# Attention block: the first chunk's k and q by seven products, the output bias from weighted rows, and a reordered first unit

## The chip, the cores and the metric

The kernel runs on one core of a Trainium2 chip. The metric is the device time of one execution in microseconds (us), as the median of several runs. The engines are TensorE (PE, its weight loads PEld), VectorE (DVE), ScalarE (ACT), GpSimd (POOL) and SyncE (SP, which only starts loads and stores here).

## The reference

The input x is 8 sequences of 1024 rows of 512 numbers, float32. With LN a layer norm without weights:

```python
def attn(x):                       # 16 heads of 32
    Q, K, V = (split_heads(x @ W.T + b) for W, b in ((Wq, bq), (Wk, bk), (Wv, bv)))
    scores = Q @ K.T / sqrt(32) - (i - j)     # causal, and a decay of 1 a step
    return merge(softmax(scores) @ V) @ Wo.T + bo
def ffn(x):                        # rotate by a Hadamard matrix, quantize to 4 bits, ternary weights
    return quantize(x @ H) @ ternary(weight).T
x = x + LN(attn(LN(x)))
x = x + LN(ffn(LN(x)))
```

The decay lets the kernel leave out keys that lie more than one block of 128 rows behind; a general path is taken if a bound on the scores (kept in `allmax`, tested at the end) does not allow that.

## The kernel before

The rows are cut into 16 chunks of 512 (`CT`), two for each sequence, and a chunk into four tiles of 128 rows. For each chunk the kernel needs the normed rows transposed (`xnT`), then k, q and v. For chunks 1 to 15 these three projections are done by a seven-product scheme for matrices cut in 2 x 2 (`class Projections`): `combine` makes sums of blocks of `xnT` in a tile `T` (two operations with `which` 0, one each with 1 and 2), `Weight.combine` and `Weight.replace` make the sums of the weights' blocks (three and two operations on POOL), `product` issues one of the seven products (four matmuls of 128x256 into one PSUM bank), and `drain` adds it from PSUM into the result, in the order `ORDER = (1, 2, 6, 7, 5, 4, 3)`. In the text k6 is k's product 6. Product 1 is drained by ACT (L440, into `u2`), the others by VectorE (L447 to L470).

Chunk 0 is done ahead of the loop, in the lines 694 to 792, by plain projections (`project`, four matmuls of 128x512 each): four of v, four of k, four of q. In between stand the preparation of the next chunk's tiles (generators `ahead_norms`: load, statistics with `rstd` on POOL, normalising on ACT as `xn`, transposing on PE), the scaling of wq on ACT (`prepare_q`), the combining of the weights on POOL, and the generator `prepare` for the feed-forward weights: their mean absolute values (`wscale`, a reduction on VectorE), for each of four blocks a comparison `below`, the ternary block `tern` and a diagonal `wdiag`; eight transposes for each pair of blocks and copies into `ternT`; a product that spreads the scales over rows (`wscale_ps`); and the output bias bo2 = bo + bv Wo, by four matmuls of `wo_sb` with bv broadcast over columns (`bvw`).

The softmax is shifted by a bound instead of a maximum. Squares of k and q (ACT) are summed per head on PE (`nk`, `nq`), the largest is taken (`mk`, `mq`), their product goes on a diagonal, a matmul with ones spreads it (`m_ps`), VectorE takes the largest (`spread`), and POOL makes the square root (pow), three roundings and the two biases (`Projections.shift`, L510 to L515). The first exponentials (L584) need this bias.

The loop goes over chunks and, in each, over eight units: four groups of four heads for each half of the chunk. A unit is `scores` (16 to 24 matmuls and four exponentials), `mask` and `add_keys` on POOL (L595, L609, in a sequence's first half also the copy L613), `values` on PE (L624 for the values, L643 for the sums by ones, which need `both` from POOL) and `divide` on VectorE. Between units stand the next chunk's products and the rest of finished tiles. The scores have one set of PSUM banks, so that a unit's scores wait for the exponentials of the unit before. Everything else on PE shares three banks (`ps_m`, class `Banks`) that go round in turn or are named by `bank`.

The order of each engine's instructions is the order of the program text (`manual_schedule`); each engine works its own queue in that order and waits at semaphores. Loads start in the order of SP's queue, which itself waits for the buffer that a load overwrites.

## Time and profile before

| what | value |
|---|---|
| median of 3 runs | 1402.89 us (1400.15 to 1403.14) |
| profiled execution | 1402.26 us, its span 1400.6 us |
| PE busy | 1364.7 us, 97% of the span |
| DVE, POOL, ACT busy | 1024.6, 907.3, 681.9 us |
| granted PE clock, mean | 0.993 |
| first k projection starts | 24.92 us |
| first scores start | 61.71 us |
| wk, wq, wf, wo: from issue to landing | 5.4, 7.9, 9.7, 12.2 us |

Times in the text are us from the span's start. The page gives for each engine its busy time and share; the windows view gives the same for a stretch of time; the timeline lists instructions with their start, duration, engine, source line (L...), operation, what is written and read, and in brackets the idle time before it and what ended it. A matmul in float32 is shown as two records, so that "x8" is four of them.

### The profile page before, as it was taken

The numbers are of one execution on the slowest core, as the hardware profiler recorded it, in microseconds if no ns is written. First come the engines' busy times: TensorE is split into PE (matmuls) and PEld (weight loads), VectorE is DVE, ScalarE is ACT, GpSimd is POOL, SyncE is SP. The second block draws the span as 40 slices with busy tenths as digits, with TensorE's granted clock in tenths as the row PEclk, the third lists the DMA queues.
The fourth block names the chain that finished last, engine by engine and source line by source line (L and its number), as shares of the span: only waits on it lengthen the run. The fifth ranks groups of instructions, "written<-read, shape, count | busy, mean of one in ns | idle before, by whom it ended". The sixth has DMA issues, their size and how long they took to land.

```text
span 1400.6 us, 34947 instructions
## 1 busy us (share of the span) xinstructions
PE 1364.7 (97%) x14472; PEld 965.8 (69%) x14472; DVE 1024.6 (73%) x2170; ACT 681.9 (49%) x1176; POOL 907.3 (65%) x1285
## 2 busy tenths in 40 slices
PE   9999999999999999999999999999999999999885
PEld 5577777767766777776776777777776777777453
DVE  5467777777777776876777777777777777687686
ACT  3345454545545445544635545454544545443443
POOL 4565758676676757657666675857657675764554
PEclk9999999999999999999999999999999999999898
DMA  6010011111011011101101101101101101100010
GB/s 227 8 47 24 25 47 46 32 39 47 24 46 47 24 47 47 47 24 47 47 24 46 47 24 47 47 25 46 47 24 47 46 25 47 32 31 17 32 39 33
DMA packets 31750, 58.23 MB, mean 42 GB/s; under 512 B 4064, under 2 KB 4448, under 8 KB 31584
## 3 DMA queue, kind: packets, MB, share of 16 engines
q1 hardware_dynamic: 30720, 54.87, 11.7%
q8 instruction: 116, 1.90, 0.6%
q10 hardware_dynamic: 864, 1.05, 0.2%
q14 instruction: 50, 0.41, 0.1%
HBM read 39.13 MB, written 16.78 MB: 40 GB/s over the span
## 4 chain that ended last, share of the span: by engine, by line


## 5 line engine op out<-in xcount | busy, mean ns | idle before, releaser
L584 ACT ACTIVATE pr<-s,bias 128x512 f32<-128x512 f32 (+1 forms) x512 | 295.8, 661 | 138.0 <-PE s L570 138.0
L609 POOL TENSOR_TENSOR both<-pr 128x1024 f32<-128x1024 f32 (+1 forms) x125 | 262.9, 2103 | 5.3
L153 PE MATMUL o_ps<-wo_sb,oT 128*128 128x512 f32 x512 | 236.5, 605 | 0.6
L595 POOL TENSOR_SCALAR_AFFINE_SELECT pr<-pr 128x1024 f32<-128x1024 f32 x128 | 150.3, 1174 | 100.2 <-ACT pr L584 96.0
L153 PEld LDWEIGHTS o_ps<-wo_sb,oT 128*128 128x128 f32 x512 | 93.2, 192 | 95.6 <-issue 92.8
L187 DVE TENSOR_TENSOR y<-o_ps,bo 128x512 f32<-128x512 f32 x64 | 44.2, 691 | 150.4 <-PE o_ps L153 150.4
L624 PE MATMUL av<-pr,v 128*32 128x128 f32 (+1 forms) x2816 | 130.7, 316 | 1.8 <-POOL pr L595 0.9
L570 PE MATMUL s<-qT,kT 32*64 32x192 f32 (+2 forms) x5632 | 120.4, 286 | 1.5 <-ACT pr L584 1.5
L570 PEld LDWEIGHTS s<-qT,kT 32*64 32x64 f32 x5632 | 100.2, 131 | 31.2 <-issue 21.8
L141 ACT ACTIVATE xn<-xc,nmr,rstd_n 128x512 f32<-128x512 f32 x60 | 48.8, 814 | 140.4 <-POOL nmr L139 140.4
L119 POOL TENSOR_SCALAR rstd_a<-mv_a 128x1 f32<-128x1 f32 x64 | 14.0, 218 | 138.9 <-DVE mv_a L127 137.6
L226 ACT ACTIVATE wT<-h_ps 128x512 f32<-128x512 f32 x64 | 38.2, 597 | 134.7 <-PE h_ps L218 134.7
L212 ACT COPY wT<-wT_ps 128x512 f32<-128x512 f32 x64 | 37.5, 586 | 129.9 <-PE wT_ps L210 129.9
L624 PEld LDWEIGHTS av<-pr,v 128*32 128x32 f32 x2816 | 74.6, 109 | 35.6 <-POOL ca L191 1.3
L238 DVE TENSOR_REDUCE sc<-h_ps 128x1 f32<-128x512 f32 x64 | 44.1, 689 | 65.1 <-ACT wT L226 65.1
L119 POOL TENSOR_SCALAR rstd_c<-mv_c 128x1 f32<-128x1 f32 x64 | 14.7, 230 | 115.3 <-DVE mv_c L127 114.5
L643 PE MATMUL av<-both,ones 128*32 128x256 f32 x1024 | 79.2, 381 | 4.5 <-POOL both L609 4.0
L285 POOL TENSOR_TENSOR y<-y,x 128x512 f32<-128x512 f32 x63 | 80.3, 1274 | 1.4 <-ACT y L284 1.3
L218 PEld LDWEIGHTS h_ps<-had_sb,wT 128*128 128x128 f32 x512 | 67.5, 194 | 6.4 <-ACT wT L212 3.4
L218 PE MATMUL h_ps<-had_sb,wT 128*128 128x128 f32 x512 | 69.0, 278 | 2.1 <-ACT wT L212 2.1
L153 PE MATMUL f_ps<-ternT,qiT 128*128 128x512 bf16 x256 | 65.8, 379 | 2.4 <-ACT qiT L257 2.4
L194 DVE SCALAR_TENSOR_TENSOR x<-y,rstd_a,xr 128x512 f32<-128x512 f32 x64 | 50.8, 793 | 16.4 <-POOL rstd_a L120 16.2
(214 smaller groups left out, 3087.9 us busy)
## 6 DMA issues: line engine op xcount, KB each, us to landing
xr<-in_x SPq DMA_DIRECT2D x64, 256.0 KB, 3.0
out<-y SPq DMA_DIRECT2D x63, 256.0 KB, 2.0
xc<-in_x SPq DMA_DIRECT2D x60, 256.0 KB, 2.8
wv_sb<-in_wvT ACTq DMA_DIRECT2D x4, 256.0 KB, 5.4
x<-in_x SPq DMA_DIRECT2D x4, 256.0 KB, 5.2
wk_sb<-in_wkT SPq DMA_DIRECT2D x1, 1024.0 KB, 5.4
wq_sb<-in_wqT SPq DMA_DIRECT2D x1, 1024.0 KB, 7.9
wf_sb<-in_wf SPq DMA_DIRECT2D x1, 1024.0 KB, 9.7
```

The costliest lines, as they stand in the source:

```text
L141: nc.scalar.activation(xn, xc, AF.Identity, bias=nmr, scale=r)
L153: nc.tensor.matmul(ps, lhs(k), rhs(k), start=(k == 0), stop=(k == KD - 1))
L187: nc.vector.tensor_tensor(y, ps, bo2, ALU.add)
L194: nc.vector.scalar_tensor_tensor(x1, y, ra, xr, ALU.mult, ALU.add)
L218: nc.tensor.matmul(xh[:, k * P : (k + 1) * P], wT[:, k, :], had_sb if k else had0_sb, start=True, stop=True,)
L285: nc.gpsimd.tensor_tensor(y2, y2, x1, ALU.add)
L570: nc.tensor.matmul(s[half * hp : (half + 1) * hp, hh, column[which] + c0 : column[which] + c1], kc.kT[hsl, g, k0 : k0 + hp], ch.qT[hsl, g, ...
L584: nc.scalar.activation(pr[:, :, r0:, own, cols], s5[:, :, r0:, own, cols], AF.Exp, bias=ch.bias[:, own, h : h + 1],)
L595: nc.gpsimd.affine_select(out=own, in_=own, compare_op=ALU.is_ge, fill=0.0, base=0, pattern=[[0, HPG], [0, 2], [1, P]], channel_multiplier=-1,
L609: engine.tensor_tensor(self.both[:, :, r0:], pr[:, :, r0:, 0, :], pr[:, :, r0:, 1, :], ALU.add)
L624: nc.tensor.matmul(av[hh * HD : (hh + 1) * HD, 0, qc : qc + w], kc.v[:, at, h * HD : (h + 1) * HD], pr[:, hh, sc : sc + w], start=(at_part ...
L643: nc.tensor.matmul(av[hh * HD : (hh + 1) * HD, 1, :], ones[:, :HD], self.both[:, hh].rearrange("p r c -> p (r c)"), start=True, stop=True, ...
```

## The change

Four things change, all at the start of the program.

1. k and q of chunk 0 are made by `Projections` like those of the other chunks: seven products each, with `T` made on VectorE, wk's and wq's block sums earlier on POOL, and wq scaled by ACT two tiles earlier. wv's block sums move behind. The steps of `prepare` are cut finer and stand between the products; the fourth tile of chunk 1 is transposed after `nq`.
2. The mean absolute values of the feed-forward weight are made by four ACT operations with an accumulated sum instead of one reduction on VectorE. The output bias is made from rows of Wo weighted by bv on POOL (seven operations) and one matmul with ones.
3. The last four operations of the first `shift` go to VectorE.
4. In chunk 0, the first tile statistics of the loop stand ahead of the first unit, and for the units 0 and 2 a product of the next chunk stands ahead of `values`.

```diff
                 elif which == 1:
-                    nc.gpsimd.tensor_tensor(self.t[:, 2], b22, b12, ALU.subtract)
+                    engine.tensor_tensor(self.t[:, 2], b22, b12, ALU.subtract)
                     self.parts[7] = self.t[:, 2]
                 else:
-                    nc.gpsimd.tensor_tensor(self.t[:, 3], self.t[:, 1], b21, ALU.subtract)
+                    engine.tensor_tensor(self.t[:, 3], self.t[:, 1], b21, ALU.subtract)
                     self.parts[4] = self.t[:, 3]
...
-            def shift(self):
+            def shift(self, engine=nc.gpsimd):
                 ch = self.ch
                 shift = small.tile([P, 1], F32, tag="shift", name=f"shift_{ch.n}")
                 nc.gpsimd.tensor_tensor(shift, spread_max(self.diag, ch.n), half1, ALU.pow)
-                nc.gpsimd.tensor_scalar(shift, shift, -SLACK, -0.5, ALU.mult, ALU.add)
-                nc.gpsimd.tensor_scalar(shift, shift, ROUND, None, ALU.add)
-                nc.gpsimd.tensor_scalar(shift, shift, ROUND, None, ALU.subtract)
+                engine.tensor_scalar(shift, shift, -SLACK, -0.5, ALU.mult, ALU.add)
+                engine.tensor_scalar(shift, shift, ROUND, None, ALU.add)
+                engine.tensor_scalar(shift, shift, ROUND, None, ALU.subtract)
                 ch.bias = small.tile([P, 2, 2], F32, tag="bias", name=f"bias_{ch.n}")
-                nc.gpsimd.tensor_scalar(ch.bias, decay_cols, shift, None, ALU.add)
+                engine.tensor_scalar(ch.bias, decay_cols, shift, None, ALU.add)
...
-        ch.kT = big.tile([P, KD, CT], F32, tag="kT", name=f"kT_{ch.n}")
-        ch.qT = big.tile([P, KD, CT], F32, tag="qT", name=f"qT_{ch.n}")
-        ch.v = big.tile([P, TPC, D], F32, tag="v", name=f"v_{ch.n}")
+        first = Projections(ch, None)
...
-        def squares_of_q(o0, o1):
-            nc.scalar.activation(sqq[:, o0:o1, :], ch.qT[:, o0:o1, :], AF.Square)
+        def squares_of(dst, blocks, cols):
+            nc.scalar.activation(dst[:, blocks, cols], ch.qT[:, blocks, cols], AF.Square)
...
-        first = Projections(ch, None)
         prep = prepare(pools, wf_sb)
-        ahead_steps = {0: "01", 1: "02", 2: "0", 3: "132", 4: "1", 5: "23", 6: "2", 7: "3", 8: "3"}
-        for i in range(3 * KD):
-            if i % 2 or not i:
-                for t in ahead_steps.get(i, ""):
-                    next(ahead_norms[int(t)])
-            which, o = divmod(i, KD)
-            if which == 0:
-                project_v(pools, wv_sb, ch.v, ch.xnT, o, ch.n)
-            elif which == 1:
-                project_qk(pools, "k", wk_sb, bk_sb, ch.kT, ch.xnT, o, ch.n)
-            else:
-                project_qk(pools, "q", wq_sb, bq_sb, ch.qT, ch.xnT, o, ch.n)
-            if i == 0:
+        def go(*which):
+            for t in which:
+                next(ahead_norms[t])
+        for t in range(TPC):
+            if t == 0:
+                go(0, 1)
+            elif t == 1:
+                go(0, 2)
+            elif t == 3:
+                go(1, 3, 2)
+            project_v(pools, wv_sb, ch.v, ch.xnT, t, ch.n)
+            if t == 0:
                 transposed(1)
                 normalised(3)
                 transposed(2)
-            elif i == 1:
+                weights[1].combine()
+            elif t == 1:
                 transposed(3)
-            elif i == KD - 1:
                 prepare_q(wq_sb)
+                weights[1].replace()
                 nc.gpsimd.tensor_tensor(bqk_step[:, 0], bq_sb[:, HB:], bq_sb[:, :HB], ALU.subtract)
                 nc.gpsimd.tensor_tensor(bqk_step[:, 1], bk_sb[:, HB:], bk_sb[:, :HB], ALU.subtract)
-                weights[2].combine()
-                weights[2].replace()
-                weights[1].combine()
-            elif i == 2 * KD - 1:
+            elif t == 2:
+                go(0)
+                for kind in range(3):
+                    first.combine(kind, nc.vector)
+            else:
                 weights[0].combine()
-                weights[1].replace()
-                sqk = squares(ch, "k", ch.kT)
-                sqq = row.tile([P, KD, CT], BF16, tag="sq", name=f"sqq_{ch.n}", bufs=1)
-            elif i == 2 * KD:
+                weights[0].replace()
+                next(prep)
+        kinds = len(Projections.ORDER)
+        first.done = kinds
+        for i in range(kinds):
+            first.product()
+            first.drain()
+            if i in (0, 2, 4):
+                go((1, 2, 3)[i // 2])
+            elif i in (1, 3):
+                go((2, 3)[i // 2])
+            next(prep)
+        sqk = squares(ch, "k", ch.kT)
+        first.done = 0
+        sqq = row.tile([P, KD, CT], BF16, tag="sq", name=f"sqq_{ch.n}", bufs=1)
+        for i in range(kinds):
+            first.product()
+            first.drain()
+            if i == 1:
                 ch.mk = largest_of(ch, "k", norms_of(ch, "k", sqk))
-            elif i == 2 * KD + 2:
-                squares_of_q(0, HB)
-            if i and i % 2 == 0:
-                for t in ahead_steps.get(i, ""):
-                    next(ahead_norms[int(t)])
-            if i in (KD, 6, 2 * KD):
+            elif i == 4:
+                squares_of(sqq, slice(0, HB), slice(0, HW))
+            elif i == 5:
+                squares_of(sqq, slice(HB, KD), slice(0, CT))
+            if i == 0:
                 next(prep)
-        squares_of_q(HB, KD)
+        squares_of(sqq, slice(0, HB), slice(HW, CT))
+        weights[2].combine()
+        weights[2].replace()
+        bank(1)
         next(prep)
+        bank(2)
         next(prep)
+        bank(1)
         ch.mq = largest_of(ch, "q", norms_of(ch, "q", [sqq[:, o, :] for o in range(KD)]))
         first.multiply()
+        bank(0)
         next(prep)
-        first.shift()
+        bank(2)
+        go(3)
+        bank(1)
+        first.shift(nc.vector)
         next(prep)
-        weights[0].replace(nc.vector)
...
+                if at == u == 0:
+                    norm = next(norms_due)
+                    steps(norm, 1)
                 new = Unit(ch, before, u)
...
-                norm = next(norms_due)
-                steps(norm, 1)
+                if at or u:
+                    norm = next(norms_due)
+                    steps(norm, 1)
...
+                late = at == 0 and u < NG
+                if not late:
+                    unit.values()
                 if u >= 4:
                     held, one, two = one, two, held
                 bank(held)
                 proj.product()
+                if late:
+                    unit.values()
                 steps(rest_b, 1)
...
-        nc.vector.tensor_reduce(ws, w, AX.X, ALU.add, apply_absolute_value=True)
+        below = row.tile([P, D], F32, tag="y", name="absolute", bufs=1)
+        for k in range(KD):
+            nc.scalar.activation(below, w[:, k, :], AF.Abs, accum_out=ws[:, k : k + 1])
         nc.vector.tensor_scalar(ws, ws, 1.0 / D, SCALE_MIN, ALU.mult, ALU.max)
...
+        def less(k):
             below = row.tile([P, D], F32, tag="y", name=f"below_{k}", bufs=1)
             nc.vector.tensor_scalar(below, w[:, k, :], lo[:, k : k + 1], None, ALU.is_lt)
+            belows[k] = below
...
-        terns = [ternary(k) for k in range(2)]
-        yield
-        for k in range(2):
-            transposed(k, terns[k])
-        terns += [ternary(k) for k in range(2, KD)]
-        yield
+        less(0)
+        yield
+        ternary(0)
+        yield
+        less(1)
+        yield
+        ternary(1)
+        transposed(0)
+        yield
+        less(2)
+        yield
+        ternary(2)
+        transposed(1)
+        yield
+        less(3)
+        bvw = row.tile([P, D], F32, tag="wT", name="bvw", bufs=1)
+        nc.gpsimd.tensor_scalar(bvw, wo_sb[:, 0, :], bvT_sb[:, 0:1], None, ALU.mult)
+        for k in range(1, KD):
+            more = row.tile([P, D], F32, tag="w", name=f"bvw_{k}", bufs=1)
+            nc.gpsimd.tensor_scalar(more, wo_sb[:, k, :], bvT_sb[:, k : k + 1], None, ALU.mult)
+            nc.gpsimd.tensor_tensor(bvw, bvw, more, ALU.add)
+        yield
+        ternary(3)
         nc.vector.tensor_copy(had0_sb, had_sb)
         nc.vector.memset(had0_sb[:, 0:1], 0.0)
-        bvw = row.tile([P, KD, P], F32, tag="wT", name="bvw", bufs=1)
-        nc.vector.tensor_copy(bvw, bvT_sb.unsqueeze(2).to_broadcast([P, KD, P]))
         yield
         pr = pools.ps_m.tile([P, D], F32, tag="pm", name="wscale_ps")
         nc.tensor.matmul(pr, ones, diag.rearrange("p k q -> p (k q)"), start=True, stop=True)
         nc.vector.tensor_copy(wscale_row, pr)
         yield
+        ps = pools.ps_m.tile([P, D], F32, tag="pm", name="bo2_ps")
+        nc.tensor.matmul(ps, ones, bvw, start=True, stop=True)
+        nc.vector.tensor_tensor(bo2, ps, bo2, ALU.add)
+        yield
+        pt = pools.ps_m.tile([P, 2, KD, P], BF16, tag="pm", name="ternT_ps_2")
         for k in range(2, KD):
-            transposed(k, terns[k])
-        yield
-        ps = pools.ps_m.tile([P, D], F32, tag="pm", name="bo2_ps")
-        for k in range(KD):
-            nc.tensor.matmul(
-                ps, bvw[:, k, :], wo_sb[:, k, :], start=(k == 0), stop=(k == KD - 1)
-            )
-            if k == KD // 2 - 1:
-                yield
-        nc.vector.tensor_tensor(bo2, ps, bo2, ALU.add)
+            for i in range(KD):
+                nc.tensor.transpose(
+                    pt[:, k - 2, i, :], terns[k][:, i * P : (i + 1) * P], ident_bf
+                )
+        yield
+        for k in range(2, KD):
+            nc.vector.tensor_copy(ternT[:, :, k * P : (k + 1) * P], pt[:, k - 2])
         yield
```

More of the change, by code (lines that the diff above doesn't have):

```diff
@@ L691, in start_rest, with bank @@
             )
+        def bank(at):
+            pools.ps_m.named = at
         x0 = big.tile([P, TPC, D], F32, tag="pr", name="x0")
@@ L814, in band @@
         rests_due = ahead(start_rest(ch, t) for ch in chunks for t in range(TPC))
-        def bank(at):
-            pools.ps_m.named = at
         held, one, two = 0, 1, 2
@@ L871, in band @@
                 new.scores()
-                unit.values()
+                late = at == 0 and u < NG
+                if not late:
+                    unit.values()
                 if u >= 4:
@@ L1189, in prepare, with ternary @@
         diag = row.tile([P, KD, P], F32, tag="u", name="wdiag", bufs=1)
-        def ternary(k):
+        belows, terns = {}, {}
+        yield
+        def less(k):
             below = row.tile([P, D], F32, tag="y", name=f"below_{k}", bufs=1)
             nc.vector.tensor_scalar(below, w[:, k, :], lo[:, k : k + 1], None, ALU.is_lt)
+            belows[k] = below
+        def ternary(k):
             tern = row.tile([P, D], BF16, tag=("qi", "qiT")[k % 2], name=f"tern_{k}", bufs=1)
             nc.vector.scalar_tensor_tensor(
-                tern, w[:, k, :], hi[:, k : k + 1], below, ALU.is_gt, ALU.subtract
+                tern, w[:, k, :], hi[:, k : k + 1], belows[k], ALU.is_gt, ALU.subtract
             )
@@ L1200, in ternary, with transposed @@
             )
-            return tern
-        def transposed(k, tern):
+            terns[k] = tern
+        def transposed(k):
             pt = pools.ps_m.tile([P, KD, P], BF16, tag="pm", name=f"ternT_ps_{k}")
             for i in range(KD):
-                nc.tensor.transpose(pt[:, i, :], tern[:, i * P : (i + 1) * P], ident_bf)
+                nc.tensor.transpose(pt[:, i, :], terns[k][:, i * P : (i + 1) * P], ident_bf)
             nc.vector.tensor_copy(ternT[:, :, k * P : (k + 1) * P], pt)
-        terns = [ternary(k) for k in range(2)]
+        less(0)
         yield
-        for k in range(2):
-            transposed(k, terns[k])
-        terns += [ternary(k) for k in range(2, KD)]
+        ternary(0)
         yield
+        less(1)
[17 more added lines that the diff above has]
+        ternary(3)
         nc.vector.tensor_copy(had0_sb, had_sb)
         nc.vector.memset(had0_sb[:, 0:1], 0.0)
-        bvw = row.tile([P, KD, P], F32, tag="wT", name="bvw", bufs=1)
-        nc.vector.tensor_copy(bvw, bvT_sb.unsqueeze(2).to_broadcast([P, KD, P]))
         yield
```

## The prediction, made before the changed kernel was run

> **What bounds the kernel now.** First the page, part 1, for the engine that is nearly always busy:

> ```profile
> PE 1364.7 (97%) x14472; PEld 965.8 (69%) x14472; DVE 1024.6 (73%) x2170; ACT 681.9 (49%) x1176; POOL 907.3 (65%) x1285
> ```

> TensorE (PE) has 36 us of idle in 1400.6. The edits touch the start alone, and the chain of waits is empty in this trace, so next come the windows of that start (columns: length, then busy us of PE, PEld, DVE, ACT, POOL):

> ```profile
> 24.90:55.50 30.60, 30.39 (x89) 14.01 (x88) 18.02 (x25) 13.19 (x20) 21.47 (x22) 1.00 0.07 20
> 55.50:61.70 6.20, 5.87 (x25) 2.66 (x23) 2.78 (x7) 1.74 (x2) 1.01 (x3) 1.00 0.00 0
> 61.70:70.20 8.50, 8.31 (x113) 6.23 (x113) 4.40 (x8) 3.80 (x8) 5.65 (x9) 1.00 0.01 3
> ```

> Row one is the k and q projections, row two the tail up to the first scores, row three the first unit. PE is full, at a granted clock of 1.00, while DVE has 12.6 us free and ACT 17.4 in row one. Work taken off PE here ends the start earlier, until another engine is late, and the loop behind, full on PE too, moves with it. Third, PE's timeline for prices:

> ```profile
> 45.20 10.46 PE L153 MATMUL q_ps<-xnT,wq_sb 128*128 128x512 f32 x24
> 55.50 1.02 PE L1221 MATMUL wscale_ps<-wdiag,ones 128*128 128x512 f32 x2
> 57.85 1.98 PE L1229 MATMUL bo_ps<-wo_sb,bvw 128*128 128x512 f32 x4
> 59.89 1.88 PE L1229 MATMUL bo_ps<-wo_sb,bvw 128*128 128x512 f32 x4
> 61.71 0.77 PE L570 MATMUL s<-qT,kT 32*64 32x192 f32 x32
> 62.41 3.72 PE L417 MATMUL q_ps<-xnT,wq_sb 128*128 128x256 f32 x16
> 68.38 1.99 PE L417 MATMUL q_ps<-T,wq_s 128*128 128x256 f32 x8
> 70.21 0.60 PE L145 MATMUL xnT_ps<-ident,xn 128*128 128x128 f32 x4
> ```

> Starts are what counts, as ends overlap. Three projections run from 45.20 to 55.50: 3.43 each. Two of the seven products run from 62.41 to 66.06 (the next scores): 1.82 each; back to back (70.64 to 72.37) 1.73. Last, what DVE pays beside POOL:

> ```profile
> 28.36 1.25 DVE L1188 TENSOR_SCALAR wscale_lo<-wscale 128x4 f32<-128x4 f32 x1
> 29.64 1.57 DVE L1193 TENSOR_SCALAR below<-wf_sb,wscale_lo 128x512 f32<-128x512 f32 x1
> 39.62 0.48 DVE L1193 TENSOR_SCALAR below<-wf_sb,wscale_lo 128x512 f32<-128x512 f32 x1
> 28.30 1.29 POOL L366 TENSOR_TENSOR wv_s<-wv_s,wv_sb 128x512 f32<-128x512 f32 x1
> 29.66 1.27 POOL L367 TENSOR_TENSOR wv_s<-wv_sb,wv_s 128x512 f32<-128x512 f32 x1
> 62.05 0.32 POOL L515 TENSOR_SCALAR bias<-decay_cols,shift 128x4 f32<-128x4 f32 x1
> 62.66 2.00 ACT L584 ACTIVATE pr<-s,bias 128x256 f32<-128x256 f32 x4 [5.18 <-PE s L570]
> ```

> The same 128x512 operation costs 0.48 alone and 1.57 beside a POOL operation of two inputs, and a 128x4 one 1.25. Drains of PSUM never vary (the group of L447: 691 to 693 ns).

> **PE's own saving.** Eight projections, 8 x 3.43 = 27.4, become 14 products at 1.77 (between 1.73 and 1.82), 24.8: 2.6 saved. The bias row's four products took (59.67 - 57.85) + (61.71 - 59.89) = 3.64; one is left, priced by the wscale product (55.50 to 56.36), 0.86: 2.8 saved. Sum 5.4, the most that can be gained. Transposes only move.

> **Up to the last k drain.** k1 starts where k started, 24.92. ACT copies v until 25.7, then does the four new Abs with sums. No row has an Abs; a Square with a sum (L226) spends 0.49 + 0.19 to the next, so 0.68 each, or 0.85 if each waits for the one before it: done at 28.4 to 29.1. The drain of k1 (0.86) is queued behind them, so its bank comes free at 29.3 to 30.0, and PE reaches k6 at 24.92 + 1.77 + 0.44 + 1.82 = 28.95: 0.7 lost.

> VectorE then has, from about 28.9 (wscale waits for Abs): seven k products' drains 5.0 (0.69 each, 0.87 for k7, 1.3 for k5's two), three tiny scalings 0.5, three below/tern/diag groups at 0.47 + 0.75 + 0.28 = 4.5, stats 0.9, two ternT copies 0.8: 11.7, ending at 40.6 without a wait. PE's own order ends k3 at 24.92 + 7 x 1.77 + 0.7 + two transposes 0.88 + two ternT sets 0.6 = 39.5, and 40.4 with k3's drain. So both are level, and VectorE's waits decide. Twelve of its operations there have two SBUF inputs or are SBUF to SBUF scalings, the kind that waited. In the trace nine of them (27.11 to 35.82) took 8.7 us for 3.5 us of work: 0.58 each. Twelve times 0.58 is 7.0, the far bound: 47.6. But POOL's long work (wq's five, 26.3 to about 33) meets the first four to six, whose delay falls before k6 ends at 31, where VectorE must wait for PE anyway; then POOL itself waits for the statistics of the fourth tile. Three more (at 39 to 41) meet the weighted rows: 3 x 0.58 = 1.7. I take 1.5 as not absorbed: the last k drain D = 42.1, between 40.6 and 47.6.

> [...]

> **From D to the first scores.** Two Squares of k 1.99 and q1's drain 0.86 stand on ACT ahead of q6: 45.0. Five products (q6 to q3) 8.9: 53.9. wscale and bias row 1.7: 55.6, which hides q3's drain (0.69) and the last Square (0.6). nq's result 0.62 later, 56.2; largest 0.69, product 0.19, diagonal 0.28: 57.4, behind which the eight ternT and the moved tile transpose (1.05) are hidden; m_ps 0.22: scores at 57.6 = D + 15.5. Before, 61.71: gain 4.1.

> **The first unit.** Before, scores to the transpose behind q6 took 70.21 - 61.71 = 8.5. After, with S the scores: m_ps, spread 0.29, pow 0.57, then four scalings on VectorE at 0.19 (L502's spacing; POOL took 61.13 to 62.37, 1.24), so bias at S + 2.0 where it was S + 0.66; exp until S + 4.1; mask, sum and copy on POOL (1.11 + 1.28 + 0.61) until S + 7.35. PE: scores 0.7, two products 3.65, scores 0.7, the product put ahead 1.82, values 0.95: the sums are reached at S + 7.8, so nothing waits. Without that reordering they would be reached at S + 6.0 and wait 1.35, so it repays the late bias, and 0.19 that the trace shows at 67.81. The product put ahead needs T of the next chunk: after bias come two ternT copies, the statistics moved in front (0.9) and T (1.3), S + 5.0, against PE at S + 5.05. Level again, and T has two SBUF inputs, beside POOL's rstd and mask: between 0 and 1.3 lost, I take 0.4. The other `late` pass and the loop: nothing.

> **Hidden at no cost.** T of the first chunk on VectorE: 2.8 plus four waits of 0.58 from 18.5, done by 23.6, due at 29. wk's five on POOL from its landing (8.23 + 5.4 = 13.6), 7.1, due at 29 and 31. wq's scaling on ACT, 2.19 from 18.5 (landed 16.6), ends 0.5 before v's copy at 21.25; any excess delays that copy's bank. Weighted rows: four one-input operations between 0.61 (L613) and 1.51 (L373) and three at 1.27, 6.3 to 9.9, from about 37, due at 54.8. wv's five behind them (7.1) end near 54, ahead of pow at 58; that cover is 4 us, and beyond it each us delays the bias. SP: the loads queued behind the third and fourth tile wait for ACT's reads near 31 and 38 (before 30.4 and 41.9), so they are no later.

> **Sum.** 4.1 - 0.4 = 3.7. The profiled execution took 1402.26 (span 1400.6 plus 1.66): 1398.6. The median shown, 1402.89, is 0.63 above it: 1399.2. A measurement of this kernel tells about 0.2%, 2.8 us.

> **Rivals.**
> Slower: VectorE becomes the bound of the k products, because each of the twelve operations pays its 0.58 and nothing absorbs it. Scores come at D + 15.5, so it decides from D = 46.2 - 0.4 = 45.8 on; at 47.6 the loss is 1.4 + 0.4 = 1.8, 1404.7. For it: the 8.7 us for 3.5 us. Against: drains don't wait, and POOL idles in the middle. Chance 0.17.
> No change: half the waits stay (D = 44.1, gain 2.1) and T's wait in the first unit is 1.3: gain 0.8, 1402.1; with one of the two, about 1401. Chance 0.15.
> All hidden: D = 40.6, no loss in the unit, gain 5.4, 1397.5. Chance 0.13. The work does leave PE, since PE's instructions in the built program show 56 products of 128x256 for 32 of 128x512, so "does nothing" isn't a rival.

> The forecast (D between 41 and 43, gain 2.8 and more) keeps 0.55. Faster 0.68, same 0.15, slower 0.17. The range runs from 1396.3 (all hidden, with 1.2 for the spread of three runs, 1400.15 to 1403.14) to 1404.2, which leaves out the far part of the slower case.

> **What would show it.** Right: first scores near 57.6; k6 starting 0.5 to 1 late after the drain of k1; the last k drain at 41 to 43; `both` of the first unit no longer waited for. Wrong: a k drain (L447 to L470) starting more than 1.5 us after its product, with below or tern ahead of it at over 1 us; D beyond 45; PE idle ahead of the first unit's products for T; ACT's Abs above 0.9 each.

## The result, and the profile after

The changed kernel took 1399.42 us (median of 9 runs, 1396.03 to 1400.46), the kernel before 1403.14 (9 runs, 1400.15 to 1403.63): ratio 0.9975, 95% interval 0.9966 to 0.9984. A second measurement gave 1398.01 (10 runs) against 1402.12 (17 runs), ratio 0.9974 (0.9965 to 0.9983). So it is faster by 0.25%, with an interval that leaves 1 out, and close to the forecast (1399.2). The profiled execution took 1398.69, its span 1397.0, which is 3.6 less than before. Only 2.7 of that is made where the change was forecast to make all 3.7.

The page's first part for the kernel after: PE is busy 6.5 us less and still fills 97%. 1.7 of the 6.5 is a spell of lower clock near 1300 us in the kernel before, and not work (see below).

```profile
PE 1358.2 (97%) x14514; PEld 974.7 (70%) x14514; DVE 1035.5 (74%) x2190; ACT 681.0 (49%) x1181; POOL 917.9 (66%) x1290
```

The windows of the start, with the bounds used for before (length, then busy us of PE, PEld, DVE, ACT, POOL):

```profile
24.90:55.50 30.60, 28.41 (x136) 23.07 (x135) 23.44 (x41) 11.41 (x22) 25.70 (x24) 1.00 0.08 23
55.50:61.70 6.20, 5.65 (x63) 4.03 (x62) 4.49 (x14) 2.12 (x5) 1.64 (x2) 1.00 0.00 0
61.70:70.20 8.50, 7.85 (x83) 5.53 (x82) 4.35 (x9) 4.79 (x10) 7.96 (x9) 1.00 0.10 34
```

In the first row PE idles 2.2 us where it idled 0.2, and VectorE and GpSimd are busier by 5.4 and 4.2: work left PE, and PE now waits a little for the other engines. PE's timeline, after:

```profile
29.57 1.97 PE L417 MATMUL k_ps<-T,wk_s 128*128 128x256 f32 x8 [0.44 <-POOL wq_s L365]
32.98 1.97 PE L417 MATMUL k_ps<-T,wk_sb 128*128 128x256 f32 x8 [1.01 <-DVE kT L447]
39.66 1.97 PE L417 MATMUL k_ps<-xnT,wk_s 128*128 128x256 f32 x8 [0.43 <-DVE u_k L466]
45.56 1.96 PE L417 MATMUL q_ps<-T,wq_s 128*128 128x256 f32 x8
58.13 0.46 PE L525 MATMUL m_ps<-diag,ones 128*128 128x128 f32 x2 [0.55 <-DVE diag L519]
58.52 0.77 PE L570 MATMUL s<-qT,kT 32*64 32x192 f32 x32
67.00 0.64 PE L643 MATMUL av<-both,ones 128*32 128x256 f32 x8 [0.64 <-POOL both L613]
67.57 0.66 PE L145 MATMUL xnT_ps<-ident,xn 128*128 128x128 f32 x4
```

Three products of k wait (k6, k7, k3), then PE runs through to `m_ps`. For k6 the profile names GpSimd's `wq_s`, but that was done at 29.25; ScalarE's drain of k1, which frees the PSUM bank, ended at 29.48, and the wait is gone in the run where that drain comes earlier (reduce_dve). The scores start at 58.52 (before 61.71, 3.19 earlier), the transpose behind them at 67.57 (70.21, 2.64 earlier): the first unit gives 0.55 back, at the sums (L643), which wait for `both`. VectorE's timeline, after:

```profile
29.39 1.25 DVE L1223 TENSOR_SCALAR wscale_lo<-wscale 128x4 f32<-128x4 f32 x1
30.67 1.57 DVE L1230 TENSOR_SCALAR below<-wf_sb,wscale_lo 128x512 f32<-128x512 f32 x1
32.16 0.68 DVE L447 TENSOR_TENSOR kT<-k_ps,u_k 128x512 f32<-128x512 f32 x1
41.97 0.68 DVE L470 TENSOR_TENSOR kT<-k_ps,u_k 128x512 f32<-128x512 f32 x1
```

This is the wait of k7: the drain of k2 (L447) stands behind a 128x4 scaling of 1.25 and a comparison of 1.57, both beside GpSimd's sums for wq. The last k drain ends at D = 42.65. And GpSimd's and ScalarE's timelines where the first unit loses:

```profile
60.49 1.99 ACT L584 ACTIVATE pr<-s,bias 128x256 f32<-128x256 f32 x4 [2.28 <-DVE bias L515]
61.97 0.57 POOL L119 TENSOR_SCALAR rstd_n<-mv_n 128x1 f32<-128x1 f32 x1 [2.40 <-DVE mv_n L127]
62.62 0.98 POOL L120 TENSOR_TENSOR rstd_n<-rstd_n,neghalf 128x1 f32<-128x1 f32 x1
63.92 1.11 POOL L595 TENSOR_SCALAR_AFFINE_SELECT pr<-pr 128x1024 f32<-128x1024 f32 x1
```

The exponentials end at 62.48, but the mask starts at 63.92: GpSimd has the three `rstd` operations of the moved statistics in its queue ahead of it, and these wait 2.40 for `mv_n`, which VectorE computes behind the bias and two copies.

**The remaining microsecond.** At the first `o_ps` the kernel after is 2.69 ahead, and matching the 128 units one by one shows 2.70 at 100 us and 3.13 at 1290 us, a slow drift of this pair (the second profile of the same kernel shows 2.86 and 2.74, so no property of the change). The rest comes near 1300 us, where the last chunk has no next products to fill PE. Before, then after:

```profile
1300.20 0.99 PE L570 MATMUL s<-qT,kT 32*64 32x192 f32 x48 [1.49 <-ACT pr L584]
1301.91 5.35 PE L153 MATMUL o_ps<-wo_sb,oT 128*128 128x512 f32 x8
```

```profile
1297.07 0.99 PE L570 MATMUL s<-qT,kT 32*64 32x192 f32 x48 [1.49 <-ACT pr L584]
1298.77 3.65 PE L153 MATMUL o_ps<-wo_sb,oT 128*128 128x512 f32 x8
```

The wait is the same, 1.49, and the same eight records take 5.35 and 3.65: the granted clock was 0.74 from 1300 to 1304 before, 1.00 after. That is 1.70 of lead, of which 1.25 goes again by 1333 (0.92 of it a wait of `wT_ps` for VectorE that the second profile hasn't). 2.70 + 0.43 + 1.70 - 1.25 = 3.58. So of the profiled pair's 3.6, 2.7 belong to the change. The fall of the clock near 1300 is in four of the 14 profiles of this case (before, shift_pool, bias4, wq_later), so it isn't the old kernel's alone. The medians differ by 3.7 and 4.1; what their further microsecond is made of isn't shown, as only single executions have a profile. More time at a lower clock in the kernel before doesn't seem to be it: in the second measurement the runs' mean granted clock averages 0.9938 for both kernels.

### The profile page after: what moved, and what is told of

Same layout as the page of the kernel before. It is cut to its first block, busy times and chain, and to the rows that moved or that the text cites. A ratio compares the mean times of both kernels' runs of the same rounds, so it can differ in the third digit from the quotient of the medians.

```text
span 1397.0 us, 35074 instructions
## 1 busy us (share of the span) xinstructions
PE 1358.2 (97%) x14514; PEld 974.7 (70%) x14514; DVE 1035.5 (74%) x2190; ACT 681.0 (49%) x1181; POOL 917.9 (66%) x1290
## 3 DMA queue, kind: packets, MB, share of 16 engines
q10 hardware_dynamic: 864, 1.05, 0.2%
## 4 chain that ended last, share of the span: by engine, by line
## 5 line engine op out<-in xcount | busy, mean ns | idle before, releaser
L584 ACT ACTIVATE pr<-s,bias 128x512 f32<-128x512 f32 (+1 forms) x512 | 295.3, 660 | 134.6 <-PE s L570 132.3
L153 PE MATMUL o_ps<-wo_sb,oT 128*128 128x512 f32 x512 | 235.5, 603 | 0.6
L153 PEld LDWEIGHTS o_ps<-wo_sb,oT 128*128 128x128 f32 x512 | 93.0, 192 | 94.8 <-issue 91.9
L570 PE MATMUL s<-qT,kT 32*64 32x192 f32 (+2 forms) x5632 | 120.5, 286 | 1.5 <-ACT pr L584 1.5
L570 PEld LDWEIGHTS s<-qT,kT 32*64 32x64 f32 x5632 | 100.3, 131 | 30.6 <-issue 20.7
L226 ACT ACTIVATE wT<-h_ps 128x512 f32<-128x512 f32 x64 | 38.2, 597 | 135.0 <-PE h_ps L218 135.0
L238 DVE TENSOR_REDUCE sc<-h_ps 128x1 f32<-128x512 f32 x64 | 44.1, 689 | 65.2 <-ACT wT L226 65.2
L643 PE MATMUL av<-both,ones 128*32 128x256 f32 x1024 | 79.2, 381 | 4.6 <-POOL both L609 4.0
L153 PE MATMUL f_ps<-ternT,qiT 128*128 128x512 bf16 x256 | 66.0, 381 | 2.4 <-ACT qiT L257 2.4
L146 ACT COPY xnT<-xnT_ps 128x512 f32<-128x512 f32 x60 | 35.2, 586 | 61.0 <-PE xnT_ps L145 61.0
```

Of the source, the lines that this page charges most:

```text
L153: nc.tensor.matmul(ps, lhs(k), rhs(k), start=(k == 0), stop=(k == KD - 1))
L238: nc.vector.tensor_reduce(sc, xh, AX.X, ALU.max, apply_absolute_value=True)
L570: nc.tensor.matmul(s[half * hp : (half + 1) * hp, hh, column[which] + c0 : column[which] + c1], kc.kT[hsl, g, k0 : k0 + hp], ch.qT[hsl, g, ...
L584: nc.scalar.activation(pr[:, :, r0:, own, cols], s5[:, :, r0:, own, cols], AF.Exp, bias=ch.bias[:, own, h : h + 1],)
L643: nc.tensor.matmul(av[hh * HD : (hh + 1) * HD, 1, :], ones[:, :HD], self.both[:, hh].rearrange("p r c -> p (r c)"), start=True, stop=True, ...
```

## The experiments

One table for all, since one reading ties them together: D is the end of the last k drain (L470's start plus its duration), and the third tile's statistics show when that tile's load landed, which differs from execution to execution (23.66 to 26.49); GpSimd's sums for wq stand behind it.

| kernel | third tile's statistics | D | first scores | scores - D | first `o_ps` | `o_ps` - scores | time, us |
|---|---|---|---|---|---|---|---|
| before | 24.00 | | 61.71 | | 93.73 | 32.02 | 1402.26 |
| after | 25.79 | 42.65 | 58.52 | 15.87 | 91.04 | 32.52 | 1398.69 |
| after, again | 26.38 | 42.46 | 58.33 | 15.87 | 90.87 | 32.54 | 1398.01, 10 runs |
| no_late | 24.90 | 42.56 | 58.43 | 15.87 | 95.33 | 36.90 | 1403.73 |
| shift_pool | 24.28 | 41.98 | 57.84 | 15.86 | 89.71 | 31.87 | 1398.30 |
| norm_back | 24.45 | 42.14 | 58.01 | 15.87 | 91.23 | 33.22 | 1397.41 |
| reduce_dve | 25.32 | 42.19 | 58.06 | 15.87 | 90.58 | 32.52 | 1397.93 |
| drain_first | 23.66 | 40.46 | 56.33 | 15.87 | 88.85 | 32.52 | 1397.50 |
| drain_first again | 25.13 | 41.01 | 56.89 | 15.88 | 89.43 | 32.54 | 1398.01, 7 runs |
| best | 24.48 | 40.95 | 56.82 | 15.87 | 88.70 | 31.88 | 1397.25, 6 runs |
| wq_later | 24.21 | 42.40 | 59.33 | 16.93 | 93.41 | 34.08 | 1402.19 |
| bias4 | 26.02 | 44.44 | 62.90 | 18.46 | 95.42 | 32.52 | 1403.38 |
| bias4_drain | 25.44 | 42.79 | 61.24 | 18.45 | 93.76 | 32.52 | 1401.47, 10 runs |
| bias_only | 26.49 | | 62.18 | | 96.70 | 34.52 | 1402.72 |

Times without a count are of one execution each and by themselves tell nothing below some 4 us, since the changed kernel scattered from 1396.03 to 1400.46. They come from different chips too: beside no_late, shift_pool, bias4 and bias_only the kernel before took 1404.81, beside drain_first, reduce_dve and wq_later 1406.38, once each. The starts repeat better: at the scores 0.2 between the changed kernel's two profiles, and D lies from 41.98 to 42.65 in the five profiles whose program is the same up to there (after, after again, no_late, shift_pool, norm_back). A shift of D below 0.7 therefore shows nothing by itself. Where the tail is as in the changed kernel, scores come 15.86 to 15.88 us after D, and where the first unit is, `o_ps` 32.52 to 32.54 after the scores. So each edit is priced by which of the columns it moves.

**no_late**: values ahead of the product in all units, as before.

```diff
-                late = at == 0 and u < NG
+                late = False
```

> The changed kernel with `values` ahead of the next chunk's product again in units 0 and 2. Markers: first scores (58.52 us in the changed kernel), the transpose behind the product put ahead (67.57), the first output projection o_ps (91.04; before 93.73). Theory A, the chain from bias over exponentials, mask and `both` sets the first unit: PE reaches the sums at about 64.6 and `both` comes at 66.95 as before, so PE waits about 2.3 there, the product comes after it, and o_ps starts 1.8 later, 92.8. In unit 2 nothing waits. Rival B, only PE's amount of work counts, order does not: o_ps stays at 91.0.

The waits came as theory A has them: 1.43 for the mask and 1.05 for `both`, against 0.64, 1.84 more. But `o_ps` came 4.29 later than in the changed kernel. PE's timeline and two windows (granted clock third from the end):

```profile
64.99 0.86 PE L624 MATMUL av<-pr,v 128*32 128x256 f32 x16 [1.43 <-POOL pr L595]
66.90 1.08 PE L643 MATMUL av<-both,ones 128*32 128x256 f32 x8 [1.05 <-POOL both L613]
67.91 3.78 PE L417 MATMUL q_ps<-T,wq_s 128*128 128x256 f32 x8
```

```profile
67.00:68.00 1.00, 1.00 (x9) 0.19 (x9) 0.00 (x0) 0.00 (x0) 1.00 (x1) 0.50 0.01 2
74.00:76.00 2.00, 2.00 (x11) 1.75 (x10) 0.88 (x2) 0.00 (x0) 0.00 (x0) 1.00 0.00 0
```

After 2.5 us of waits within 3.3 us the clock was at a half from 66.4 to 73.2, and a product took 3.78 instead of 1.99. That is the other 2.5 us. The 1.84 belong to the edit; a fall of the clock came behind such waits in some executions and not in others (near 1300, behind the same wait of 1.49, in one and not in another; see the last section), so the 2.5 are of this execution.

**shift_pool**: part 3 undone, all of the first bound on GpSimd.

```diff
-        first.shift(nc.vector)
+        first.shift()
```

> The changed kernel with the four last operations of the first shift on GpSimd again. Theory A: four operations at 1.24 in all (61.13 to 62.37 in the kernel before) instead of 0.79 (59.61 to 60.40): bias, exponentials, mask and `both` come 0.5 later, the wait for `both` grows from 0.64 to 1.1 and o_ps starts at 91.5. Rival B, the exponentials are covered by the two products in front of them: o_ps stays at 91.0.

`o_ps` came 1.33 earlier than in the changed kernel, beyond both. 0.67 of it is D, though the program up to there is the same (the load came 1.5 earlier; that this is the reason isn't shown), and 0.65 lies in the unit: 31.87 against 32.52.

```profile
62.59 1.11 POOL L595 TENSOR_SCALAR_AFFINE_SELECT pr<-pr 128x1024 f32<-128x1024 f32 x1 [0.46 <-ACT pr L584]
65.88 0.61 PE L643 MATMUL av<-both,ones 128*32 128x256 f32 x8
```

With the bias off VectorE, the statistics there end 1.9 us after the scores' start (3.35 in the changed kernel), GpSimd's `rstd` is done before the exponentials end, and the mask waits for them alone; the sums wait for nothing. The bias itself comes 0.76 later after `m_ps` than on VectorE, which costs 0.31 at the next scores, less than the 0.64 saved. `best` below repeats the 31.88. Part 3 loses 0.65 us in the first unit.

**norm_back**: the moved statistics back behind the first unit's product.

```diff
-                if at == u == 0:
-                    norm = next(norms_due)
-                    steps(norm, 1)
...
-                if at or u:
-                    norm = next(norms_due)
-                    steps(norm, 1)
+                norm = next(norms_due)
+                steps(norm, 1)
```

> The changed kernel with one thing undone: the first tile statistics of the loop stand behind the first unit's product again, as before; the bias is still finished on VectorE. Theory (POOL's three rstd operations, queued ahead of the mask and waiting for statistics that stand behind the bias on VectorE, are what makes `both` late): the mask starts within 0.2 us of the end of the first exponentials, the sums of the first unit (L643) no longer wait for `both`, and from the first scores to the first o_ps it takes 31.8 to 32.0 us, as with the bias on POOL (31.87), where the changed kernel took 32.52. Rival (the late bias itself does it): L643 still waits 0.5 us or more and the stretch stays at 32.4 or more.

Half of each. The mask starts 0.07 after the exponentials and the sums don't wait, as the theory has it, but the stretch is 33.22 where the theory had 31.8 to 32.0; the rival's 32.4 or more is met, for another reason than the rival's:

```profile
62.05 1.11 POOL L595 TENSOR_SCALAR_AFFINE_SELECT pr<-pr 128x1024 f32<-128x1024 f32 x1 [2.98 <-ACT pr L584]
67.33 0.66 PE L145 MATMUL xnT_ps<-ident,xn 128*128 128x128 f32 x4 [1.04 <-ACT xn L141]
```

`rstd` now comes behind the copy L613, so that the normalised tile is late, and PE waits 1.04 for that. The wait for `both` had been the price of an early tile. So the queue's order does hold up `both`, and the statistics must still be early: the bias in front of them on VectorE is the piece to move.

**bias4**: the bias row by four matmuls, as before; its seven GpSimd operations go.

```diff
...
-        nc.tensor.matmul(ps, ones, bvw, start=True, stop=True)
+        for k in range(KD):
+            nc.tensor.matmul(
+                ps, bvw[:, k, :], wo_sb[:, k, :], start=(k == 0), stop=(k == KD - 1)
+            )
```

> The changed kernel with the output bias by four matmuls and the broadcast copy again; nothing of the weighted rows on GpSimd. PE gets 3 x 0.86 = 2.6 more ahead of nq, GpSimd loses seven operations (38.9 to 49.9). Theory A: first scores at 61.1, less what VectorE's operations after 39 no longer wait (up to 0.8): 60.3 to 61.1, and o_ps at 92.8 to 93.6, so that nearly the whole gain of the change is gone. Rival C, the three waits of PE in the k products are what GpSimd's rows cost, and without them it comes out even: o_ps within 0.5 of 91.0.

4.38 later at the scores, neither the 1.8 to 2.6 of the theory nor the rival's even time. The table splits it: 2.59 lie between D and the scores (18.46 against 15.87), which is PE's own part, and 1.79 in D. wv's sums now stand where the weighted rows stood, and `below`, `tern` and `wdiag` ahead of the last drain take 0.98, 1.16 and 1.28 where they took 0.48, 0.74 and 0.63: 1.57 of the 1.79. `o_ps` is 1.69 later than in the kernel before: without the new bias row the rest of the change loses.

**bias4_drain**: the same with the drain of k2 first (as in drain_first below), to see if the mended order takes the 1.79 away.

> The changed kernel with the bias row by four matmuls again (bvw broadcast, as before) and with the drain of k2 ahead of the scalings and the first comparison. It tells what the 4.4 us of the first edit alone were made of. Theory (2.6 us are PE's three further products, and 1.8 the collisions that wv's earlier POOL operations bring to the drains ahead of k7 and k3; the mended order takes these away): k7 waits under 0.2 us, the last k drain ends at 40.5 to 41.5, the first scores start 2.5 to 3.0 us behind those of the kernel with the mended order alone (56.33 and 56.89), at 59.1 to 59.9, and the first o_ps at 91.6 to 92.4: 0.5 to 1.5 us slower than the changed kernel. Rival (wv's operations collide with whatever stands there): scores at 60.6 or later, o_ps at 93.1 or later, as slow as the kernel before.

The theory fell. k7 doesn't wait, but D is 42.79 against 41.01 of the same order with weighted rows: 1.78 again. VectorE's timeline:

```profile
37.68 1.76 DVE L1236 SCALAR_TENSOR_TENSOR tern<-wf_sb,wscale_hi,below 128x512 bf16<-128x512 f32 x1
39.36 1.28 DVE L1239 TENSOR_SCALAR wdiag<-ident,wscale 128x128 f32<-128x128 f32 x1
```

The same two in drain_first_again, where the weighted rows stand beside them:

```profile
37.36 0.74 DVE L1236 SCALAR_TENSOR_TENSOR tern<-wf_sb,wscale_hi,below 128x512 bf16<-128x512 f32 x1
38.02 0.63 DVE L1239 TENSOR_SCALAR wdiag<-ident,wscale 128x128 f32<-128x128 f32 x1
```

GpSimd's three sums for wv (37.63 to 41.90) stand beside the first pair: 1.67 more, ahead of the last two drains. The bias row in its new form is worth 4.35 us here, 2.57 on PE and 1.78 by what it keeps off VectorE. With the old row, seven products and all, the kernel is within 0.1 us of the one before at `o_ps` (93.76 and 93.73), and 0.999 of its time (0.998 to 0.9999).

**bias_only**: the kernel before with the weighted rows and one matmul, nothing else.

```diff
-        bvw = row.tile([P, KD, P], F32, tag="wT", name="bvw", bufs=1)
-        nc.vector.tensor_copy(bvw, bvT_sb.unsqueeze(2).to_broadcast([P, KD, P]))
+        bvw = row.tile([P, D], F32, tag="wT", name="bvw", bufs=1)
+        nc.gpsimd.tensor_scalar(bvw, wo_sb[:, 0, :], bvT_sb[:, 0:1], None, ALU.mult)
+        for k in range(1, KD):
+            more = row.tile([P, D], F32, tag="w", name=f"bvw_{k}", bufs=1)
+            nc.gpsimd.tensor_scalar(more, wo_sb[:, k, :], bvT_sb[:, k : k + 1], None, ALU.mult)
+            nc.gpsimd.tensor_tensor(bvw, bvw, more, ALU.add)
...
-        for k in range(KD):
-            nc.tensor.matmul(
-                ps, bvw[:, k, :], wo_sb[:, k, :], start=(k == 0), stop=(k == KD - 1)
-            )
-            if k == KD // 2 - 1:
-                yield
+        nc.tensor.matmul(ps, ones, bvw, start=True, stop=True)
+        yield
```

> The kernel before with the weighted rows and one matmul for the output bias, nothing else of the change. 2.6 less on PE behind nq. Theory A: first scores come 2.1 earlier (59.6; m_ps then waits 0.5 for the diagonal), but bias only 0.5 earlier, so the sums of unit 0 wait about 2.2 for `both` where they waited 0.19, and o_ps starts 0.5 to 0.8 earlier than 93.73, at 93.0 to 93.2. Rival B, PE's work counts: o_ps at 91.2 to 91.6.

3.0 later than before at `o_ps`, where a gain was expected. The rows end at 60.54 on GpSimd, `bo_ps` waits 0.21 for them. Half of the row's matmuls had stood between `m_ps` and the scores; with them gone the scores follow `m_ps` at once and the exponentials come 3.47 after the scores' start instead of 0.95, as the bias's operations on GpSimd take 2.29 beside VectorE's work on wq and T where they took 1.24. The next scores wait 1.09, the mask's and the sums' waits are 0.41 and 1.05. That makes the stretch from scores to `o_ps` 34.52, 2.5 of the 3.0. The late load is in the other 0.5. With it (26.49 against 24.00) VectorE's ternary steps and GpSimd's sums come 2.5 later, and PE waits where the kernel before did not:

```profile
37.15 0.40 PE L1206 MATMUL ternT_ps<-ident_bf,tern 128*128 128x128 bf16 x4 [0.68 <-DVE tern L1195]
45.91 0.39 PE L333 MATMUL nk<-sqk,head_rows 128*32 128x512 bf16 x2 [1.44 <-ACT sqk L346]
46.86 0.39 PE L333 MATMUL nk<-sqk,head_rows 128*32 128x512 bf16 x2 [0.55 <-ACT sqk L346]
```

These 2.67 take away all of the 2.6 that PE saved, and GpSimd's rows end late for the same reason. So what the row alone is worth in the kernel before, this one execution doesn't show.

**drain_first**, twice: k2's drain ahead of the scalings and the first comparison, the ternary steps one product later.

```diff
-            next(prep)
+            if i:
+                next(prep)
...
-            if i == 0:
+            if i in (0, 2):
                 next(prep)
...
             nc.scalar.activation(below, w[:, k, :], AF.Abs, accum_out=ws[:, k : k + 1])
+        yield
...
-        yield
 
         def less(k):
```

> The changed kernel with the drain of k2 ahead of the scalings and the first comparison on VectorE, and all steps of the ternary weights one product later. In the changed kernel k7 waited 1.01 for that drain and the last k drain ended at 42.65. Theory A, VectorE's work and its waits beside GpSimd set the end of the k products: k7's wait goes, another drain is late in its place, the last k drain ends at 42.2 to 43.2, first scores at 58.1 to 59.1. Rival B, the one badly placed drain is the loss: last k drain 1.0 earlier, first scores at 57.5.

> The drain of k2 ahead of the scalings and the first comparison, once more and timed. Theory (the order on VectorE makes the gain): last k drain ends at 40.3 to 41.2 and k7 does not wait, whatever the load of the third tile does; about 2 us faster than the changed kernel. Rival (the earlier landing, 23.66 against 25.79, made half of it): with a landing near 25.8 the last k drain ends at 41.3 to 42.0, and the time is 1 us faster or less.

D is 40.46 and, with a later load, 41.01: 1.5 to 2.2 earlier than in the changed kernel's two profiles, about 1.0 or more earlier than in any profile with the old order, and k7 doesn't wait in either. Theory A of the first run fell, and its rival's direction was right with twice the size. The repeat is 1.45 earlier than the changed kernel on the same chip; that the earlier load of the first run made its other half isn't shown. VectorE's timeline of the repeat:

```profile
29.35 0.69 DVE L447 TENSOR_TENSOR kT<-k_ps,u_k 128x512 f32<-128x512 f32 x1 [3.31 <-ACT u_k L440]
31.43 1.38 DVE L1231 TENSOR_SCALAR below<-wf_sb,wscale_lo 128x512 f32<-128x512 f32 x1
40.33 0.68 DVE L470 TENSOR_TENSOR kT<-k_ps,u_k 128x512 f32<-128x512 f32 x1
```

The comparison still takes 1.38, with no drain behind it that PE waits for. But the median is the same as the changed kernel's, 1398.01, where the theory had 2 us less. In its profiled execution the lead of 1.44 at `o_ps` is 0.97 from 760 us on, and the rest goes past 1350, where the granted clock was 0.88 and 0.95 in two windows of 10 us, against 1.00 in the changed kernel. Whether the other six runs lost it in the same way isn't known.

**reduce_dve**: one reduction on VectorE instead of four operations on ScalarE.

```diff
-        for k in range(KD):
-            nc.scalar.activation(below, w[:, k, :], AF.Abs, accum_out=ws[:, k : k + 1])
+        nc.vector.tensor_reduce(ws, w, AX.X, ALU.add, apply_absolute_value=True)
```

> The changed kernel with the mean absolute values by one reduction on VectorE instead of four Abs on ScalarE. VectorE is free from 26.7 to 28.8 in the changed kernel; the reduction took 2.25 in the kernel before, so the scalings start at 29.0 instead of 28.78. The drain of k1 is no longer queued behind Abs: k6's wait of 0.5 goes. Theory A, VectorE is the bound: last k drain ends between 42.6 and 43.0, first scores at 58.5 to 58.9. Rival B, ScalarE's queue is the bound: first scores 0.5 earlier, 58.0.

0.46 earlier at the scores, as the rival has it: k6 no longer waits 0.44, k7 waits 1.42 instead of 1.01. The reduction (2.25) fits into VectorE's idle time ahead of the first drain. D scatters by up to 0.7 for one and the same program, so the 0.44 at k6 is shown and what it leaves at the scores is not.

**wq_later**: wq's five sums on GpSimd behind the fifth product of k.

```diff
             else:
-                weights[0].combine()
-                weights[0].replace()
                 next(prep)
...
+            if i == 4:
+                weights[0].combine()
+                weights[0].replace()
             if i in (0, 2, 4):
```

> The changed kernel with wq's five block operations on GpSimd behind the fifth k product, so that GpSimd does nothing long from 28 to 37 and everything behind it comes later. Theory A, the waits of VectorE are GpSimd's operations: the second tiny scaling and the first comparison, 1.25 and 1.57 in the changed kernel, take 0.17 and 0.48, k7 no longer waits, and the k drains up to k5 end about 1.5 earlier; GpSimd, pushed back by about 7, has wv's operations in front of the square root, which starts 4 to 5 later than the largest is ready, and first exponentials move behind 64. Rival C, those durations are VectorE's own (a cold start, a write of four numbers): they stay at 1.25 and 1.57.

The three scalings and the comparison take 0.17, 0.17, 0.16 and 0.49, where they took 0.49, 0.17, 1.25 and 1.57: GpSimd's sums made those times. In this run's timeline of VectorE:

```profile
28.90 0.16 DVE L1224 TENSOR_SCALAR wscale_lo<-wscale 128x4 f32<-128x4 f32 x1
29.09 0.49 DVE L1231 TENSOR_SCALAR below<-wf_sb,wscale_lo 128x512 f32<-128x512 f32 x1
```

The sums then collide further on (D 42.40), and push wv's behind `spread`: pow starts at 61.36, `m_ps` had waited 1.53, the clock fell to 0.50 from 59.6 to 63.0, and `o_ps` came 2.4 later. The first exponentials start at 62.84, not behind 64 as expected.

**best**: drain_first, reduce_dve and shift_pool together.

> The changed kernel with three edits together: the drain of k2 ahead of the scalings and the first comparison (ternary steps one product later), one reduction on VectorE instead of four operations on ScalarE for the mean absolute values, and the first shift on GpSimd. Theory (the gains seen one by one come from the edits: 2.2, 0.5 and 0.65 us at the first o_ps): o_ps at 88.0 to 88.8, about 2.5 to 3 us faster than the changed kernel. Rival (part of the gains was the landing of the third tile's load, which came 1.5 to 2.1 us earlier in two of those executions and moves POOL's operations on wq with it): where that load lands as in the changed kernel's profile (statistics at 25.8), o_ps comes at 89.5 or later and the kernel is at most 1.5 us faster.

D 40.95, unit 31.88: `o_ps` at 88.70, 2.2 earlier than the changed kernel's on the same chip, of which reduce_dve adds next to nothing once the drain is first (40.95 against 41.01). The rival's condition (a load near 25.8) wasn't met. The median is 1397.25, ratio to before 0.9967 (0.9955 to 0.9979), the lowest median here, but only 0.8 below the changed kernel's, with overlapping intervals: the 2.5 to 3 us that the theory had are not there. The profiled spans differ by 2.0.

> The changed kernel itself, on the chip of the two others. Theory (its gain at the first o_ps, 2.7 us, is its own): o_ps between 90.0 and 91.5, and 2.5 to 3.7 us faster than the kernel before. Rival (the landing of the third tile's load moves the end of the start by half its shift, in both kernels): o_ps leaves that range by as much as the landing differs from 25.79, up to 1 us either way.

The changed kernel again came within 0.2 of its first profile at `o_ps`, with the load 0.6 later: by this the rival fell. The gain of 4.1 in the medians lies above the 2.5 to 3.7 that the theory had.

## Why the prediction was right, and where its steps failed

The size was right at 1399.2 against 1399.42, but not for all its reasons: the gain in the start was 2.7, not 3.7, and a microsecond from elsewhere, which the prediction didn't have and the runs don't explain, filled the gap. That was luck.

**PE's saving.** The bias row was put at 2.8 and measured 2.58 (18.45 - 15.87). Products start 1.73 to 1.80 apart, as taken. What the sum didn't have is that the row's GpSimd form keeps wv's two-input sums away from VectorE, 1.8 more. What the seven products' 2.6 came to is not shown, as no run undid them alone; with the old row (bias4, bias4_drain) all the other parts together left `o_ps` 1.69 later than before, or even.

**Up to the last k drain.** D was put at 42.1, between 40.6 and 47.6; it is 42.65 and 42.46. (With D at 40.6 the prediction's own sum would give a gain of 5.6; its 5.4 is PE's saving.) k6 waited 0.44 (0.7 forecast). The spread over single operations was off: the first collisions were counted as absorbed before PE needs VectorE, yet two of them (1.25 and 1.57) stood ahead of k2's drain and cost 1.01 at k7, while the middle was as empty as forecast. This is one of the prediction's own signs of being wrong: k2's drain started at 32.16, 3.0 after its product's end, with a comparison of 1.57 ahead of it. D still came out near 42.1, since the three operations at 39 to 41, put at 1.7 of delay, had 0.35 (`wdiag` 0.63 for 0.28). The rival that VectorE becomes the bound, deciding from D = 45.8, was not met in any run; the worst, 44.44, had wv's sums in that place. Had each of the twelve operations waited for a whole GpSimd sum of 1.27, D would have been 40.6 + 12 x 1.27 = 55.8, an estimate that the same 44.44 refutes; delays close to that length did occur (1.57 for 0.48, beside sums of 1.27), but few.

**From D to the scores.** 15.5 was forecast, 15.87 measured in nine profiles to 0.01. q6 at D + 2.91 and the bias row fit; the term too small is the end of it, from the largest over `diag` to the scores, 1.73 instead of 1.4 (two hand-overs between VectorE and PE, and `m_ps` at 0.39 instead of 0.22). Together with D the scores are 0.92 late.

**The first unit: the step that failed.** The bias came at S + 1.9 (2.0 forecast), the exponentials ended at S + 4.0 (4.1), and T was not waited for, with q6 issued at S + 5.06 (5.05): the 0.4 put there was not paid. But mask, sum and copy ended at S + 8.4 and not at S + 7.35, and "nothing waits" was wrong: L643 waited 0.64. The moved statistics were priced on VectorE alone. Their three `rstd` operations moved too, on GpSimd's queue, past the first mask. The size was nearly made good by the two errors together, 0.55 lost for 0.4. The reordered products are worth more than the 1.35 that was forecast: without them (no_late) 1.84 more of waits, and 4.3 with the clock at 0.50 behind those.

**Cover.** wv's sums were to end near 54 with 4 us before pow; they ended at 56.57 with 2.4, as the weighted rows took 11.1 (38.88 to 49.95) where 9.9 was the most that was put. wq_later, where they ended at 61.39, shows the price when that cover is gone: scores 1.06 later after D, and a fall of the clock to 0.50.

## What to carry to other kernels

An instruction that frees something on the critical path should be issued ahead of work that can be delayed by another engine: the comparison, at 1.4 to 1.6 us in both orders, cost PE 1.0 in front of the drain of k2 and nothing behind it. When a step is moved, follow every queue it issues to, and ask what each instruction overtakes; a step's cost on its main engine says nothing on the one that must finish it. And compare kernels at a marker near the edit before comparing their times: a constant like the 15.87 separates edits that scatter of some 4 us in whole runs hides.

## What the runs showed of the hardware that was not expected

```profile
1298.49:1301.90 3.41, 1.44 (x57) 1.09 (x53) 2.78 (x8) 2.99 (x6) 2.85 (x4) 1.00 0.29 96
1301.91:1305.31 3.40, 3.40 (x7) 1.46 (x5) 0.00 (x0) 2.23 (x5) 1.91 (x1) 0.50 0.14 55
```

```profile
1294.76:1298.17 3.41, 1.81 (x72) 1.19 (x61) 2.48 (x8) 2.99 (x6) 2.88 (x3) 1.00 0.20 74
```

  PE was busy 1.44 of 3.41 us ahead of the fall, and 1.81 where none came: there the grid cuts the waits in two. In no_late it was 1.46 (62.96 to 66.37), and the fall came; in bias_only the waits lie in two steps with 1.91 and 2.36, and none came. Counted over all 14 traces, each of the 31 steps at full clock with PE busy for at most 1.53 us was followed by half clock; with 1.54 to 1.59 us it was 6 of 12, and above that one of more than 5000 (wq_later, 56.17 to 59.57, 1.87). This is a count over these traces; why the one came isn't known.
- A 128x4 operation on VectorE took 0.16 or 1.25, a 128x512 `tern` 0.72 to 1.76, and it was what GpSimd ran beside it that made the difference: with wq's sums moved away (wq_later) the 1.25 was 0.16, and the 1.76 beside wv's sums (bias4_drain) was 0.74 beside the weighted rows (drain_first again). The delay goes the other way too: the weighted row beside `tern` at 40.44 took GpSimd 2.08 in the changed kernel, against 1.56 with VectorE idle in bias_only.
- Absolute values with an accumulated sum on ScalarE came 0.76 us apart for 128x512, between the 0.68 of a square with a sum (0.49 + 0.19) and the prediction's 0.85, which was an estimate.
